# Graph network on one core: in the last layer one block of nodes passes from gathering to multiplication

## The chip, the cores and the metric

The kernel runs on one core of one Trainium2 chip. The metric is the device time of one execution in microseconds (us). The time before is 2127.4 us, the median of 3 runs (2123.55 to 2129.25).

## The reference

6250 nodes with 256 features (C) each, 100,000 edges from `src` to `dst`, random and sorted by `dst`. In short:

```python
h = relu(layernorm(x))                       # N = 6250, C = 256
y = h
for l in range(3):                           # three layers
    a = y + segment_sum(y[src], dst, N)      # each node adds up its neighbours
    a = relu(a @ W1s[l] + b1s[l])
    a = relu(a @ W2s[l] + b2s[l])
    y = a @ W3s[l] + b3s[l]
a = y + segment_sum(y[src], dst, N)          # the head, the last layer
a = relu(a @ cW1 + cb1)
a = relu(a @ cW2 + cb2)                      # cW2 is 256 x 64
return x + a @ cW3 + cb3                     # cW3 is 64 x 256
```

Everything is float32.

## The kernel before

**Blocks and layers.** The nodes are cut into 49 blocks of 128 (the last one holds 106). After a preparation (sorting the edges' indices, layernorm, a first split of the features) there are four layers, the head being the last. In each, every destination block needs the sum over its neighbours, its aggregate, which is made in one of two ways.

**Gathered blocks.** The edges of a block lie in 17 index columns of 128. For each column POOL issues one indirect DMA (`rows<-table,idx`, L1407) that fetches 128 rows of the layer's features from a table in memory. When all 17 are there a *visit* follows: 23 TensorE matmuls (46 records in the trace, since float32 is done in two passes) `sums<-rows,hot`, L1446, which add the rows up by destination with the help of one-hot matrices (`hot`, L1430, from DVE). DVE adds the sums to the node's own features (`u<-u,sums`, L1475), TensorE turns the result (L1506), and ACT adds the first bias and applies the relu. (The first weight of each layer is already in the features that are summed, since a sum and a matmul commute: the third weight of a layer has been multiplied with the first of the next.)

**Multiplied blocks.** For other blocks the kernel holds a count matrix, 6250 sources by 128 destinations, in uint8. It is cast to fp32r in strips (`a<-at`, by ACT and DVE in turn) and multiplied with the features, which lie in the tile `XY` for all 49 source blocks, split into a high and a low half. Four blocks together make a panel (L1700: 196 matmuls of 512 columns); a single block is multiplied "by node" (L1622: 49 matmuls, the strip being the stationary operand). Which block goes which way is told by `panels`, by `gone` (blocks that can be gathered) and by `solos`, the single blocks that a later layer multiplies. The first layer gathers 23 blocks and multiplies 26 by node; the second and third multiply seven panels and block 19 and gather 20 blocks; the last multiplies seven panels and blocks 18 and 19 and gathers 19.

**Building the matrices.** The 30 count matrices (blocks 18 to 47) are built once, during the first layer, in the order `made`. Each takes 16 *build steps* (GSUB): two matmuls `bp<-hi,lo` (L1094) of one-hot tiles that DVE makes (`lo` and `hi`, both L1053; one pair serves two steps, each has two buffers) and one copy of the counts into the uint8 tile `at`, by ACT (L1102) and DVE (L1104) in turn. A finished matrix is stored to memory (`mats`) for the later layers. There are three `at` tiles; a matrix is begun only when the casts of the one three places before it are written.

**Turns.** Products are written in turns, one strip of the matrix each: 13 a block by node, 49 a panel. Before a turn's matmuls stands whatever is due: a visit, a piece of a small network, and in the first layer up to three build steps, as far as an evenly rising list of goals asks and the buffers allow (`product_by_node`):

```python
goal = min(goals[at - PRE], built[0] + 3)
while built[0] < goal and free_of(built[0] // GSUB - 3):
    next(beside); built[0] += 1
```

**The plan of the gathers.** The order is fixed when the program is written. A planned clock adds up what TensorE is to do (`clock`, with prices for columns, visits and build steps). For each layer `work_of` estimates the work; the plan ends `TAIL[l]` planned us before that work does, and the gathers are spread evenly up to there (`pace`). Each gather waits on POOL for a matmul of its planned moment. A visit stands where the clock reaches its time, or, at the latest, `LATE[l]` turns past the layer's last turn (negative: before it):

```python
self.end = begun[self.l] + work_of(self.l) - TAIL[self.l]
self.pace = (self.end - clock[0] - MARGIN) / self.upto[-1]
...
return now[0] >= ends[self.l] + LATE[self.l] or clock[0] >= self.first + (
    self.upto[self.done + 1] - self.upto[1]) * self.pace
```

**The small networks.** For four blocks at a time (block 48 alone) there are two more matmuls, the *seconds* and the *thirds*. Before the head these are L1256 and L1313; in the head the seconds are `ps<-h,w`, L1248 for four blocks and L1256 for one, the thirds `ps<-clT,h`, L1268 for four and L1310 for one. In the head the input x is added: it is loaded into `xt` (L521, the load issued by SP; L1284 zeroes the tile first where block 48 does not fill it), DVE adds the bias to it (L1287) and the product (`zz`, L1297), and SP stores `zz`. For the last panel, blocks 44 to 47, the inputs are fetched ahead into `rows` tiles and L1280 adds the bias. The tile `clT` served the builds and is used again later as space (`spare`): for single blocks' aggregates and for the bias row, so that L1268, L1287 and L1310 name it as an operand.

**The queues.** Each engine takes its instructions in program order. Loads of matrices, of x and all stores are issued on SP's queue, gathers on POOL's.

Of the kernel before, what the change touches and what calls it, by code (L numbers as in the profile page):

```python
# [10 lines left out]
U8 = mybir.dt.uint8  # L11
# [6 lines left out]
P = 128  # L18
# [378 lines left out]
def sorted_edges(  # L397
# [39 lines left out]
    N, C = x.shape  # L437
    (E,) = src.shape
    NLAYER = W1s.shape[0]
# [27 lines left out]

    gone = [(0, 4), (4, 4), (8, 4), (12, 4), (16, 4), (44, 4), (48, 1)]
    panels = [(20, 4), (24, 4), (28, 4), (32, 4), (36, 4), (40, 4), (44, 4)]
    solos = [[], [19], [19], [18, 19]]  # L470
    stock = panels + [(b, 1) for b in max(solos, key=len)]
    place_of = {b + i: (p, i) for p, (b, n) in enumerate(stock) for i in range(n)}
    S0 = 2 * min(place_of)
# [3 lines left out]
    made = [b + i for b, n in teams for i in range(n)]  # L477
    for i in range(panels[-1][1]):
        made.insert(6 * i + 5, panels[-1][0] + i)
    assert sorted(made) == sorted(place_of) and sum(gone[-3]) == panels[0][0] and gone[-2] == panels[-1] and all(n == gone[0][1] for _, n in gone[:-1]) and sorted(  # L480
        b + i for b, n in gone[:-2] + gone[-1:] + panels for i in range(n)) == list(range(NT))
    NQ = len(gone)
# [498 lines left out]
    with tc.manual_schedule():  # L981
        with tc.tile_pool(name="prep", bufs=2) as prep, tc.tile_pool(
            name="ps_t", bufs=2, space=PSUM
# [374 lines left out]
        class Gathered:  # L1358
# [23 lines left out]
            def meets(self):  # L1382

                if self.first is None or self.done == self.n or now[0] < self.rest:
                    return False
                return now[0] >= ends[self.l] + LATE[self.l] or clock[0] >= self.first + (
                    self.upto[self.done + 1] - self.upto[1]) * self.pace

            def begin(self):
                self.one_hots(0)  # L1390
                self.end = begun[self.l] + work_of(self.l) - TAIL[self.l]
                self.pace = (self.end - clock[0] - MARGIN) / self.upto[-1]
# [121 lines left out]
        EARLY = 8  # L1514
        PRE = (GSUB + EARLY) // 2
        tails = [7] + [panels[-1][1] + gone[-1][1]] * (NLAYER - 1) + [panels[-1][1]]
        order = [[]] + [[0, 1, 2, 19, 3, 4, 5, 6]] * 2 + [[0, 1, 18, 2, 3, 19, 4, 5, 6]]
        order = [[p if p < len(panels) else place_of[p][0] for p in o] for o in order]
        nodes = [b + i for b, n in teams for i in range(n)]
        parts = [(j, 1) for j in range(NT)]  # L1520
# [11 lines left out]
        spare = clT.rearrange("p a q s -> p (a q s)").bitcast(F32)  # L1532
        sums = ps_g.tile([P, W], F32, name="sums")
        MARGIN = 6.0
        TAIL = [10.0] + [-5.0] * (NLAYER - 1) + [10.0]
        LATE = [-8] + [10] * (NLAYER - 1) + [-8]
        COLS, FULL32, TURN, VISIT, BUILD, BURST = 0.457e-3, 1.68e-3, 0.4, 3.0, 0.2, 0.3
        clock = [0.0]
        FAR, SPAN = 7, 6
# [9 lines left out]
        def work_of(l):  # L1549

            t = (len(nodes) if l == 0 else sum(stock[p][1] for p in order[l])) * NT * W * COLS
            t += len(layers[l].blocks) * (len(ROUNDS) * VISIT + TURN)
            for k, n in ((l, NT - tails[l]), (l - 1, tails[l - 1])):
                mid = NOUT if k == NLAYER else C
                t += (k >= 0) * n * (P * KC + C) * FULL32 * (2 if mid == C else 0.5)
            t += 2 * (len(gone) + (len(teams) if l == 0 else len(panels)) - 1) * BURST
            if l == 0:
                t += BUILD * GSUB * len(made) + TURN * len(nodes)
            return t
# [44 lines left out]
        def product_by_node(l, bs, ps_a, us, beside):  # L1604
            begun.setdefault(l, clock[0])
            aggs = [ps_a.tile([P, W], F32, name="agg") for _ in bs]
            for j0, m in solo_parts if l else node_parts[pieces.index(bs)]:
                at = now[0]
                tick(open_one(l))
                open_one(l).advance()  # L1610
                if beside is not None:
                    goal = min(goals[at - PRE], built[0] + 3)
                    while built[0] < goal and free_of(built[0] // GSUB - 3):
                        next(beside)
                        built[0] += 1
                prepare(at + 1 + (AHEAD if l == 0 else AHEAD + 2))
                a = ring.pop(at)
                for j in range(j0, j0 + m):
                    assert l == 0 or (l, j) in fresh
                    for i, agg in enumerate(aggs):  # L1620
                        d = (i * m + j - j0) * P
                        mm = nc.tensor.matmul(agg, a[:, d:d + P], XY[:, j, :], start=(j == 0),  # L1622
                                              stop=(j == NT - 1))
                        passed(W * COLS, mm)
                    if l == 0 and bs == pieces[-1]:
                        seen(l, j)

            def halves():
                for u, agg in zip(us, aggs):
                    nc.scalar.copy(u, agg[:, :C])  # L1630

            def whole():
                for u, agg in zip(us, aggs):
                    nc.vector.tensor_tensor(u, u, agg[:, C:], OP.add)  # L1634

            later(1, halves)
            later(2, whole)
# [39 lines left out]
        def product(l, p, ps_a):  # L1677
            b0, n = stock[p]
            if n == 1:
                k = solos[l][::-1].index(b0)  # L1680
                u = alone[l, b0] = late.tile([P, C], F32, name="us", bufs=1) if (
                    k == 1) else spare[:, k // 2 * C:(k // 2 + 1) * C]
                return product_by_node(l, (b0,), ps_a, [u], None)
            last = len(panels) - 1
            w = n * P
            begun.setdefault(l, clock[0])
            agg = [ps_a.tile([P, W], F32, name="agg") for _ in range(KC)]
            for at, j in enumerate(c * CH + i for c in CHUNKS for i in range(CH)):
                u = now[0]
                tick(open_one(l))  # L1690
                open_one(l).advance()
                if l == NLAYER and p == last and at == NT - 3:
                    bring_inputs(b0, n)
                prepare(u + 1 + AHEAD + 2)
                a = ring.pop(u)
                assert (l, j) in fresh, (l, j, now[0], ends[l - 1], [k for k in range(NT) if (l, k) not in fresh], len(queue), layers[l - 1].done)
                for c in range(KC):
                    for half in range(2):
                        o = half * C + c * P
                        mm = nc.tensor.matmul(agg[c][:, :w], XY[:, j, o:o + P], a[:, :w],  # L1700
                                              start=(at == 0 and half == 0),
                                              stop=(at == NT - 1 and half == 1))
                    passed(2 * w * COLS, mm)
                if p == last:
                    seen(l, j)
            h1 = work.tile([P, KC, W], F32, name="h1", bufs=2)
            hurry = p == last
            for c in range(KC):
                if hurry and c:
                    nc.vector.tensor_scalar(h1[:, c, :w], agg[c][:, :w], b1[l][:, c:c + 1], 0.0,  # L1710
                                            op0=OP.add, op1=OP.max)
                else:
                    nc.scalar.activation(h1[:, c, :w], agg[c][:, :w], AF.Relu,  # L1713
                                         bias=b1[l][:, c:c + 1])
            mlp(l, b0, n, h1, hurry, FAR)
# [12 lines left out]
        with tc.tile_pool(name="hots", bufs=1) as hots, tc.tile_pool(  # L1728
            name="ats", bufs=1
        ) as ats, tc.tile_pool(name="rings", bufs=AHEAD + 2) as rings, tc.tile_pool(  # L1730
            name="gath", bufs=24
        ) as gath, tc.tile_pool(
            name="ps_a", bufs=2, space=PSUM
        ) as ps_a, tc.tile_pool(name="ps_b", bufs=3, space=PSUM) as ps_b:
            begun = {0: clock[0]}
            rings.tile([P, 64], U8, name="align", bufs=1)
            layers[0].begin()
            layers[0].send(8)
            beside = build(hots, ats, ps_b)
            while now[0] < PRE:  # L1740
                for _ in range(2):
                    next(beside)
                    built[0] += 1
                tick(layers[0])
                layers[0].advance()
            later(1, lambda: later(2, lambda bad=verdict(): judge(bad)))
            for team in teams:
                product_of_team(*team, ps_a, beside, team == teams[-1])
            assert next(beside, None) is None and built[0] == total
        chunks = ctx.enter_context(tc.tile_pool(name="chunks", bufs=1))  # L1750
        late = ctx.enter_context(tc.tile_pool(name="late", bufs=1))
        rings = ctx.enter_context(tc.tile_pool(name="rings2", bufs=AHEAD + 5))
        rings.tile([P, 128], U8, name="align", bufs=1)
        gath = ctx.enter_context(tc.tile_pool(name="gath2", bufs=27))
        ps_a = ctx.enter_context(tc.tile_pool(name="ps_a2", bufs=4, space=PSUM))
        for l in range(1, NLAYER + 1):
# [67 lines left out]
```

## Time and profile before

| | |
|---|---|
| median of 3 runs | 2127.4 us |
| the profiled execution's own time | 2128.1 us |
| its span | 2126.3 us |
| PE (TensorE matmul) busy | 2034.3 us, 96% |
| PEld (weight load) busy | 1495.9 us, 70% |
| DVE busy | 925.0 us, 44% |
| ACT busy | 872.8 us, 41% |
| POOL busy | 1445.9 us, 68% |
| gathers (L1407) | 1394, 996 ns each on POOL |
| products: panels (L1700), by node (L1622) | 978.6 us, 405.4 us of PE |
| visits (L1446) | 248.3 us of PE, 33.5 us idle before them |
| build matmuls (L1094) | 128.3 us of PE, 14.9 us idle before them |

A view of a stretch gives window, length, and then the busy time of PE, PEld, DVE, ACT and POOL (with the number of instructions), the mean granted TensorE clock, the DMA engines' busy share and GB/s. A view of waits gives, for a group, its idle time in us, how many waits, and the longest. A timeline row gives start, duration, engine, line, operation, tiles (out<-in), number of instructions, and in brackets the idle time before it and what ended it. The first layer's products by node run from 150 to 689 us; the second layer's gathers begin at 714 us, the third's at 1195, the last's at 1668; the last product ends at 2116. What stands ahead of 150 us is the preparation.

### The profile page before, as it was taken

The page shows a single profiled execution, that of the slowest core. Times are in us where ns is not written, and L with a number is a line of the kernel's source. Part 1 is how long each engine was busy: PE and PEld are TensorE (multiplying, and loading weights), DVE is VectorE, ACT ScalarE, POOL GpSimd, SP SyncE. Part 2 cuts the span into 40 slices and gives each one's busy share as a digit, 9 for nine tenths or more (in the row PEclk, how much of TensorE's full clock was granted, in tenths as well). Part 3 has the DMA queues.
Part 4 walks back from the last instruction along what each step waited for, and adds up shares of the span by engine and source line. Part 5 has one row for each costly group of instructions (what it writes and reads, how often), then busy time and mean ns, then how long its engine had stood idle before and what let it go on. Part 6 is the DMA issues. An engine that isn't in the chain of part 4 may idle for free.

```text
span 2126.3 us, 33236 instructions
## 1 busy us (share of the span) xinstructions
PE 2034.3 (96%) x12076; PEld 1495.9 (70%) x12076; DVE 925.0 (44%) x2103; ACT 872.8 (41%) x1793; POOL 1445.9 (68%) x1467
## 2 busy tenths in 40 slices
PE   6889999999999999999999999999999999989998
PEld 4657676667676777777777777777776767766665
DVE  6987767677662422232234322322233323223333
ACT  5766656456555433323233423232233322222222
POOL 3747777677774477777777477777776477777772
PEclk9989999999999999999999999999999999999999
DMA  5534455545455654555566554555555555555563
GB/s 174 159 117 148 145 156 150 157 139 162 140 161 168 205 163 145 160 177 161 154 184 202 171 165 149 176 166 158 169 171 176 173 170 185 161 184 185 154 189 109
DMA packets 184900, 347.54 MB, mean 163 GB/s; under 512 B 32446, under 2 KB 118496, under 8 KB 184726
## 3 DMA queue, kind: packets, MB, share of 16 engines
q0 software_dynamic: 68960, 185.36, 29.9%
q1 hardware_dynamic: 113838, 158.12, 22.8%
q8 instruction: 96, 1.57, 0.3%
q10 hardware_dynamic: 1928, 1.85, 0.3%
q14 instruction: 78, 0.64, 0.1%
HBM read 287.93 MB, written 57.26 MB: 162 GB/s over the span
## 4 chain that ended last, share of the span: by engine, by line
PE 86%; DMA 4%; DVE 3%; issue 1%; ACT 1%; POOL 1%; DVEq 0%; SPq 0%; POOLq 0%; ACTq 0%
PE agg L1700 43%; PE agg L1622 15%; PE sums L1446 11%; PE ps L1256 6%; PE ps L1313 6%; PE bp L1094 4%; DMA rows<-table,idx 4%; PE ps L1506 1%; DVE hi L1053 1%; POOL rows L1407 1%; DVE at L1104 1%; PE ps L1268 1%; PE ps L1248 0%; DVE lo L1053 0%; ACT at L1102 0%
## 5 line engine op out<-in xcount | busy, mean ns | idle before, releaser
L1407 POOL DMA_INDIRECT rows<-table,idx x1394 | 1388.8, 996 | 595.7 <-issue 225.7
L1700 PE MATMUL agg<-a,XY 128*128 128x512 f32 x4116 | 978.6, 395 | 1.9 <-DVE clT L1634 1.9
L1700 PEld LDWEIGHTS agg<-a,XY 128*128 128x128 f32 x4116 | 764.9, 188 | 192.7 <-issue 35.0
L1598 ACT CAST a<-at 128x512 fp32r<-128x512 uint8 (+1 forms) x542 | 328.7, 617 | 653.7 <-PE agg L1700 613.1
L1598 DVE CAST a<-at 128x512 fp32r<-128x512 uint8 x543 | 246.8, 456 | 515.7 <-PE agg L1700 479.1
L1622 PE MATMUL agg<-XY,a 128*128 128x512 f32 x1470 | 405.4, 410 | 1.7 <-ACT a L1582 1.0
L1622 PEld LDWEIGHTS agg<-XY,a 128*128 128x128 f32 x1470 | 260.0, 190 | 51.4 <-issue 6.6
L1446 PE MATMUL sums<-rows,hot 128*32 128x256 f32 x3772 | 248.3, 391 | 33.5 <-DMA rows<-table,idx 33.3
L1446 PEld LDWEIGHTS sums<-rows,hot 128*32 128x32 f32 x3772 | 124.0, 111 | 151.0 <-DMA rows<-table,idx 46.1
L1582 ACT CAST a<-at 128x512 fp32r<-128x512 uint8 (+2 forms) x362 | 197.2, 576 | 6.6 <-PE agg L1622 6.6
L1102 ACT CAST at<-bp 128x392 uint8<-128x392 f32 x252 | 121.5, 490 | 186.9 <-PE bp L1094 181.3
L1104 DVE CAST at<-bp 128x392 uint8<-128x392 f32 x228 | 128.6, 564 | 137.4 <-PE bp L1094 135.0
L1475 DVE TENSOR_TENSOR u<-u,sums 128x256 f32<-128x256 f32 x82 | 34.4, 419 | 301.3 <-PE agg L1700 273.6
L1094 PE MATMUL bp<-hi,lo 128*128 128x196 bf16 x960 | 128.3, 256 | 14.9 <-DVE hi L1053 13.3
L1313 PE MATMUL ps<-w,h 128*128 128x256 f32 x588 | 133.8, 379 | 1.4 <-ACT h L1259 0.9
L1053 DVE TENSOR_TENSOR hi<-cols,pairs 128x784 bf16<-128x784 bf16 x240 | 134.9, 562 | 0.0
L1256 PE MATMUL ps<-h,w 128*128 128x512 f32 (+3 forms) x332 | 133.8, 545 | 0.3 <-ACT h L1713 0.3
L1094 PEld LDWEIGHTS <-lo 128*128 128x128 bf16 x960 | 72.3, 100 | 83.5 <-DVE hi L1053 34.9
L1313 PEld LDWEIGHTS ps<-w,h 128*128 128x128 f32 x588 | 111.3, 190 | 18.5 <-ACT h L1259 1.4
L1321 DVE TENSOR_TENSOR zz<-ps,w 128x512 f32<-128x512 f32 (+1 forms) x75 | 50.2, 679 | 116.5 <-PE ps L1313 116.5
L1053 DVE TENSOR_TENSOR lo<-lanes,pairs 128x512 bf16<-128x512 bf16 x240 | 100.6, 419 | 0.7 <-issue 0.3
L1510 ACT ACTIVATE h<-ps,bias 128x256 f32<-128x256 f32 (+1 forms) x116 | 47.6, 464 | 128.5 <-PE ps L1506 128.5
(170 smaller groups left out, 962.6 us busy)
## 6 DMA issues: line engine op xcount, KB each, us to landing
at<-mat SPq DMA_DIRECT2D x151, 448.0 KB
mat<-at SPq DMA_DIRECT2D x30, 784.0 KB
rows<-table,idx POOLq DMA_INDIRECT x1394
table<-zz SPq DMA_DIRECT2D x72, 256.0 KB
back<-table SPq DMA_DIRECT2D x99, 128.0 KB
xs<-in_x_dram SPq DMA_DIRECT2D x8, 768.0 KB
table<-zs SPq DMA_DIRECT2D x24, 256.0 KB
out_dram<-zz SPq DMA_DIRECT2D x24, 256.0 KB
```

The lines of the kernel that those rows point to most:

```text
L1053: nc.vector.tensor_tensor(o.rearrange("p q (n t) -> p q n t", t=2), values.rearrange("p (n t) -> p n t", t=2)[:, None, :, :].to_broadcast( ...
L1094: mm = nc.tensor.matmul(bp[:, m * HW:(m + 1) * HW], lo[:, q + m, :], hi[:, q + m, :], start=True, stop=True)
L1102: nc.scalar.copy(o, v)
L1104: nc.vector.tensor_copy(o, v)
L1256: mm = nc.tensor.matmul(ps[:mp, :w], weights[l][0][:, c, i * P:i * P + mp], h1[:, c, :w], start=(c == 0), stop=(c == KC - 1))
L1313: mm = nc.tensor.matmul(o, h2[0][:, c, nodes], w3[:, c, :], start=(c == 0), stop=(c == KC - 1))
L1407: got = nc.gpsimd.indirect_dma_start(out=t, out_offset=None, in_=tables[self.l][:, :], in_offset=bass.IndirectOffsetOnAxis(ap=idx[:, o:o + ...
L1446: nc.tensor.matmul(self.sums[m * Q:(m + 1) * Q, :C], self.hot[:, c - min(rounds), m, :], self.rows[g, c + 4 * m], start=(c == ROUNDS[0][0] ...
L1582: nc.scalar.copy(a[:, i * m * P:(i + 1) * m * P].rearrange("p (j d) -> p j d", j=m), counts[b][:, j:j + m, :])
L1598: cast(o, at[:, :, d:d + m * P])
L1622: mm = nc.tensor.matmul(agg, a[:, d:d + P], XY[:, j, :], start=(j == 0), stop=(j == NT - 1))
L1700: mm = nc.tensor.matmul(agg[c][:, :w], XY[:, j, o:o + P], a[:, :w], start=(at == 0 and half == 0), stop=(at == NT - 1 and half == 1))
```

## The change

In the last layer block 17 is no longer gathered but multiplied by itself, as blocks 18 and 19 already are: 18 blocks are gathered and three multiplied singly. Its count matrix is built in the first layer, as the 27th of now 31 (`made.insert(26, 17)`). In the last layer's order its product stands after the first panel and block 18's after the second. `work_of` counts the added product, the visit that goes and the added build steps of itself. Four numbers of the plan change: the first layer's plan ends 16 planned us before its work (10 before), the last layer's 3 us after it (10 before it), and the last layer's last visit is forced 5 turns ahead of the products' end instead of 8. The aggregate of the third single block takes another slot of `spare`. `clT` grows by 128 bytes a partition for the two half blocks of 17, and the alignment tiles are changed to suit.

```diff
     panels = [(20, 4), (24, 4), (28, 4), (32, 4), (36, 4), (40, 4), (44, 4)]
-    solos = [[], [19], [19], [18, 19]]
+    solos = [[], [19], [19], [17, 18, 19]]
...
         made.insert(6 * i + 5, panels[-1][0] + i)
+    made.insert(26, 17)
...
-        order = [[]] + [[0, 1, 2, 19, 3, 4, 5, 6]] * 2 + [[0, 1, 18, 2, 3, 19, 4, 5, 6]]
+        order = [[]] + [[0, 1, 2, 19, 3, 4, 5, 6]] * 2 + [[0, 17, 1, 18, 2, 3, 19, 4, 5, 6]]
...
-        TAIL = [10.0] + [-5.0] * (NLAYER - 1) + [10.0]
-        LATE = [-8] + [10] * (NLAYER - 1) + [-8]
+        TAIL = [16.0] + [-5.0] * (NLAYER - 1) + [-3.0]
+        LATE = [-8] + [10] * (NLAYER - 1) + [-5]
...
                 u = alone[l, b0] = late.tile([P, C], F32, name="us", bufs=1) if (
-                    k == 1) else spare[:, k // 2 * C:(k // 2 + 1) * C]
+                    k == 1) else spare[:, 3 * (k // 2) * C:(3 * (k // 2) + 1) * C]
...
-            rings.tile([P, 64], U8, name="align", bufs=1)
+            rings.tile([P, 192], U8, name="align", bufs=1)
...
-        rings.tile([P, 128], U8, name="align", bufs=1)
```

How the builds stand in the first layer is seen on ACT, around the last strip of the fourteenth block's product. `a<-at` 128x512 is one turn's cast, `at<-bp` is ACT's half of the evictions, so one for every two build steps, `pairs` begins half a matrix, and `un` takes up a finished product. (Lines of the changed kernel count one more here.) Before:

```order
L1582 COPY a<-at 128x128
L1048 COPY pairs<-clT 128x64
L1102 COPY at<-bp 128x49x8
L1582 COPY a<-at 128x512 x2
L1102 COPY at<-bp 128x49x8
L1582 COPY a<-at 128x512
L1630 COPY un<-agg 128x256
L1102 COPY at<-bp 128x49x8
L1582 COPY a<-at 128x512
L1102 COPY at<-bp 128x49x8
```

The same place of the changed kernel:

```order
L1583 COPY a<-at 128x512 x6
L1583 COPY a<-at 128x128
L1049 COPY pairs<-clT 128x64
L1103 COPY at<-bp 128x49x8 x2
L1583 COPY a<-at 128x512
L1103 COPY at<-bp 128x49x8
L1583 COPY a<-at 128x512
L1103 COPY at<-bp 128x49x8
L1049 COPY pairs<-clT 128x64
L1103 COPY at<-bp 128x49x8
```

Before, evictions and casts alternate nearly one to one; now seven casts stand without an eviction, and then five evictions follow with two casts among them.

The end of the last layer on PE: `agg<-a,XY` are the last panel's products, `sums<-rows,hot` the last visit, `ps` the small networks, `h_...` their operands (a number is only the tile's own). Before:

```order
L1248 MATMUL ps<-h_20413,w_16837 64x256 x4
L1700 MATMUL agg<-a,XY 128x512 x12
L1268 MATMUL ps<-clT,h_20534 128x256 x4
L1700 MATMUL agg<-a,XY 128x512 x12
L1256 MATMUL ps<-h_20522,w_16837 64x128 x2
L1700 MATMUL agg<-a,XY 128x512 x8
L1310 MATMUL ps<-clT,h_20595 128x256
L1700 MATMUL agg<-a,XY 128x512 x20
L1248 MATMUL ps<-h_20651,w_16837 64x256 x4
L1268 MATMUL ps<-clT,h_20654 128x256 x4
```

And now, from the last visit on:

```order
L1447 MATMUL sums<-rows,hot 32x256 x23
L1701 MATMUL agg<-a,XY 128x512 x8
L1507 MATMUL ps<-ident,u 128x128 x2
L1701 MATMUL agg<-a,XY 128x512 x4
L1249 MATMUL ps<-h_20600,w_16940 64x256 x4
L1701 MATMUL agg<-a,XY 128x512 x12
L1269 MATMUL ps<-clT,h_20715 128x256 x4
L1257 MATMUL ps<-h_20705,w_16940 64x128 x2
L1311 MATMUL ps<-clT,h_20763 128x256
L1249 MATMUL ps<-h_20742,w_16940 64x256 x4
L1269 MATMUL ps<-clT,h_20779 128x256 x4
```

From the last visit on 24 product matmuls remain where 64 did, and the thirds of blocks 16 to 19, the seconds and thirds of block 48 now stand behind the last product.

On DVE, at the same place, before:

```order
L1287 TENSOR_TENSOR xt<-xt,clT 128x512 x2
L1598 COPY a<-at 128x512
L1297 TENSOR_TENSOR zz<-ps,xt 128x512 x2
L1598 COPY a<-at 128x512 x2
L1284 MEMSET xt 128x256
L1287 TENSOR_TENSOR xt<-xt,clT 128x256
L1297 TENSOR_TENSOR zz<-ps,xt 128x256
L1710 TENSOR_SCALAR h_20651<-agg,bias 128x512
L1280 TENSOR_TENSOR rows<-rows,clT 128x256 x4
L1297 TENSOR_TENSOR zz<-ps,rows 128x256 x4
```

And now:

```order
L1711 TENSOR_SCALAR h_20742<-agg,bias 128x512
L1288 TENSOR_TENSOR xt<-xt,clT 128x512 x2
L1298 TENSOR_TENSOR zz<-ps,xt 128x512 x2
L1285 MEMSET xt 128x256
L1288 TENSOR_TENSOR xt<-xt,clT 128x256
L1298 TENSOR_TENSOR zz<-ps,xt 128x256
L1281 TENSOR_TENSOR rows<-rows,clT 128x256 x4
L1298 TENSOR_TENSOR zz<-ps,rows 128x256 x4
```

The relu of the last product (`h<-agg,bias`) now stands ahead of the adds of blocks 16 to 19 and of block 48, and all of these follow the last product.

## Prediction

> **What bounds the kernel now.** I read the page, then busy time by stage, the visits (the 46 "sums" records of one gathered block), PE's waits, POOL's gathers and the timeline of the first layer.
>
> ```profile
> 163.00:640.00 477.00, 468.53 (x3208) 330.39 (x3208) 337.10 (x763) 281.61 (x636) 349.04 (x349) 1.00 0.50 150
> 1690.00:2098.00 408.00, 381.66 (x2323) 279.24 (x2322) 124.02 (x253) 113.59 (x202) 303.41 (x306) 0.98 0.56 173
> ```
> Columns: window, length, busy PE, PEld, DVE, ACT, POOL, granted clock, DMA share, GB/s. In the first layer (upper row) PE is busy 98% and DVE 71%. In the last layer PE loses 26 us, and its clock is under 1.00.
>
> ```profile
> 730.00:1174.00 444.00, 56.56 (x920) 28.98 (x920) 1.00 0.56 170
> 1210.00:1642.00 432.00, 58.57 (x920) 29.66 (x920) 1.00 0.55 168
> 1690.00:2098.00 408.00, 66.57 (x874) 31.42 (x874) 0.98 0.56 173
> ...
> PE sums L1446 <- DMA rows<-table,idx: 26.0, 11, 6.2
> ...
> PE sums L1446 <- DMA rows<-table,idx: 4.9, 3, 1.7
> ...
> 1865.17 0.63 PE L1446 MATMUL sums<-rows,hot 128*32 128x256 f32 x6
> 1871.99 5.16 PE L1446 MATMUL sums<-rows,hot 128*32 128x256 f32 x40 [6.19 <-DMA rows<-table,idx]
> ...
> 1872.00:1877.00 5.00, 5.00 (x40) 2.12 (x40) 0.00 (x0) 0.00 (x0) 2.40 (x3) 0.51 0.67 231
> ```
> The first three rows are PE's time in visits (second, third, last layer). The second layer's 20 cost 56.56/20 = 2.83 us each. The last layer's 19 should take 53.8; they took 66.57 and waited 26.0 besides, so 38.8 us are lost to late rows. A third of that is no idle time: after a wait of 6.19 the other 40 matmuls took 5.16 us, at a granted clock of 0.51. The third layer lost 58.57 - 56.6 + 4.9 = 6.9.
>
> [...]
>
> Why rows are late:
>
> ```profile
> 714.25 4.41 POOL L1407 DMA_INDIRECT rows<-table,idx  x1 [43.75 <-ACT XY L1185]
> ...
> 1170.56 2.80 PE L1446 MATMUL sums<-rows,hot 128*32 128x256 f32 x46
> ...
> 1194.88 1.28 POOL L1407 DMA_INDIRECT rows<-table,idx  x1 [26.13 <-PE agg L1700]
> ...
> 1636.37 0.63 PE L1446 MATMUL sums<-rows,hot 128*32 128x256 f32 x6
> ...
> 1668.41 0.95 POOL L1407 DMA_INDIRECT rows<-table,idx  x1 [31.85 <-PE agg L1700]
> 1669.66 0.95 POOL L1407 DMA_INDIRECT rows<-table,idx  x1 [0.30 <-issue]
> ...
> 2091.71 0.97 POOL L1407 DMA_INDIRECT rows<-table,idx  x1 [0.31 <-issue]
> ...
> 2094.35 2.80 PE L1446 MATMUL sums<-rows,hot 128*32 128x256 f32 x46
> ```
> A gather costs POOL 0.95 + 0.30 = 1.25 us at best. From the last layer's first gather to its last visit PE has 2094.35 - 1668.41 - 38.8 = 387 us of work for 323 gathers: 1.20 each, which POOL cannot follow. The same for the layers of 20 visits and 340 gathers: (1636.37 - 1194.88 - 6.9)/340 = 1.28 in the third (loss 6.9), (1170.56 - 714.25)/340 = 1.34 in the second (none).
>
> **Last layer.** The product of block 17 is added: 49 matmuls, as this one of block 18.
>
> ```profile
> 1762.61 8.12 PE L1622 MATMUL agg<-XY,a 128*128 128x512 f32 x35
> ...
> 1772.11 3.49 PE L1622 MATMUL agg<-XY,a 128*128 128x512 f32 x14
> ```
> That is +11.4 us after overlap at the ends. A visit goes, -2.8, with its 17 gathers. Casts and `mat` loads of the new product lie beside PE: DVE and ACT are busy 124 and 114 of 408 us there. PE's work up to the last visit becomes 405 us, since the visit now stands 24 product matmuls ahead of the end where 64 stood: 405/306 = 1.32 a gather, against POOL's 1.25. Between the third layer's loss and the second's none, nearer the latter, I keep 2 us (ends 0 and 8). So the stall gives -36.8.
>
> **The end.** Three pieces of MLP that stood among the last panel's products now follow them: thirds of blocks 16 to 19 (1.13), seconds and thirds of block 48 (0.65, 0.70). The products end 2.5 us earlier for it. What follows them gets longer:
>
> ```profile
> 2107.86 0.27 DVE L1284 MEMSET xt<- 128x256 f32 x1
> 2108.16 0.76 SPq L521 DMA_DIRECT2D xt<-in_x_dram  x2
> ...
> 2110.41 0.43 DVE L1287 TENSOR_TENSOR xt<-xt,clT 128x256 f32<-128x256 f32 x1 [2.27 <-DMA xt<-in_x_dram]
> ...
> 2111.51 4.85 PE L1700 MATMUL agg<-a,XY 128*128 128x512 f32 x20
> 2111.61 0.42 DVE L1297 TENSOR_TENSOR zz<-ps,xt 128x256 f32<-128x256 f32 x1 [0.78 <-PE ps L1310]
> ...
> 2116.47 0.75 DVE L1710 TENSOR_SCALAR h<-agg,bias 128x512 f32<-128x512 f32 x1 [4.43 <-PE agg L1700]
> 2117.13 1.42 DVE L1280 TENSOR_TENSOR rows<-rows,clT 128x256 f32<-128x256 f32 x4
> 2119.72 1.42 DVE L1297 TENSOR_TENSOR zz<-ps,rows 128x256 f32<-128x256 f32 x4 [1.17 <-PE ps L1268]
> ```
> Before, DVE's last add ends at 2121.14, 4.8 us after the products (2116.36), and the kernel 5.2 later. Now, in DVE's order, there stand behind the products: 0.75 (h), two pairs of adds of blocks 16 to 19 (2 x 1.29), MEMSET 0.27, the wait for block 48's x (2.28 from the MEMSET's end), 0.43, 0.42, and the two groups of four (2 x 1.42): 9.7 us with the first 0.1, +4.9. The load of x is issued only after that MEMSET and, on SP, behind two stores of blocks 16 to 19, so about 1 more (an estimate; ends 0 and 3): +5.9.
>
> **First layer.** The 31st matrix is 16 build steps more (two bp matmuls, half of DVE's `lo` and `hi`, one eviction). In 13 turns a block, PE and DVE look like this:
>
> ```profile
> 327.49 3.01 PE L1622 MATMUL agg<-XY,a 128*128 128x512 f32 x12
> ...
> 330.34 0.69 PE L1094 MATMUL bp<-hi,lo 128*128 128x196 bf16 x6
> ...
> 331.71 0.95 DVE L1430 TENSOR_TENSOR hot<-colf,rel 128x768 f32<-128x768 f32 x1
> 331.82 0.34 PE L1094 MATMUL bp<-hi,lo 128*128 128x196 bf16 x2
> 333.06 0.56 DVE L1104 CAST at<-bp 128x392 uint8<-128x392 f32 x1
> 333.19 0.51 PE L1094 MATMUL bp<-hi,lo 128*128 128x196 bf16 x4 [1.03 <-DVE hi L1053]
> ...
> 334.34 0.56 DVE L1104 CAST at<-bp 128x392 uint8<-128x392 f32 x1
> 334.50 0.51 PE L1094 MATMUL bp<-hi,lo 128*128 128x196 bf16 x4
> ...
> 335.62 0.56 DVE L1104 CAST at<-bp 128x392 uint8<-128x392 f32 x1
> ...
> PE bp L1094 <- DVE hi L1053: 7.2, 12, 1.4
> ```
> Three turns without a step take PE 330.34 - 327.49 = 2.85, 0.95 each; one with two steps 1.31 (333.19 to 334.50). A step is thus 0.18 of PE, and the matrix 16 x 0.18 = +2.9. DVE needs 1.28 for two steps (one eviction to the next, back to back), 0.64 a step. A turn of two steps fits (1.28 in 1.31); one of three asks 1.92 of DVE against 0.95 + 3 x 0.18 = 1.49 of PE. The two turns of three that begin at 330.34 end at 334.50: 4.16 instead of 2.98, 0.59 lost a turn.
>
> Before, 8 of the layer's turns have three steps; counted over the whole order, now 69 have, in runs of up to 10, behind runs without any. The goal rises faster, the builder stops at its third buffer and then catches up three steps a turn. It is no more DVE work than 12 us, but it is bunched: in the empty turns DVE cannot work ahead, as `lo` and `hi` have two buffers. So 61 more such turns cost between 0.43 (DVE's bare rate) and 0.59 (measured, with a `hot` in between) each, 26 to 36 us; where a visit or MLP lies in the run PE waits less, which stretches the lower end to 15. I take 0.57, 35 us: in long runs DVE has its other work to do too.
>
> The layer's last visit was forced two planned microseconds after its last gather:
>
> ```profile
> 668.05 0.63 PE L1446 MATMUL sums<-rows,hot 128*32 128x256 f32 x6
> 671.07 4.46 PE L1446 MATMUL sums<-rows,hot 128*32 128x256 f32 x40 [2.38 <-DMA rows<-table,idx]
> ```
> It lasts 668.05 to 675.53, 7.5 instead of 2.8. With the plan ending sooner 8 lie between: -4.6. The second and third layers keep their order: 0. The 128 bytes by which tiles move: 0, as nothing in the trace depends on them.
>
> **Sum.** 2.9 + 35 - 4.6 - 36.8 + 11.4 - 2.8 - 2.5 + 5.9 = +8.5. The profiled execution took 2128.1 (span 2126.3), 0.7 over the median of the runs, 2127.4; from the median: 2136.
>
> **Rivals.**
> Bunching costs less: the runs of three fall beside visits and MLPs, whose 2.8 to 3.5 us of PE let DVE catch up. At 15 to 26 us the kernel takes 2116 to 2127. For it: 30% of PE's time in that layer is no product. Against: the runs stand in turns with products alone at least as often.
>
> Faster, because DVE has room: at 71% busy and 12 us more it stays under 74%, so the steps are absorbed wherever they stand. With the bursts at 5 or less, 2136 - 30 = 2106. It decides below 20 us of new waits for `hi`. [...] Against it stands DVE back to back for the 1.28 us above, with PE waiting for it in a layer whose mean is 71%.
>
> Gathers stay late: bulk loads share the DMA engines, and a row asked for in a full stretch lands late although POOL has time. In the visit at 1865.17 PE waited beyond 1871 for gathers sent before it. At the third layer's 6.9 or a little more, and a tail 3 us longer, 2143 to 2149.
>
> **Chances.** Forecast (2130 to 2142) 0.52; less bunching 0.23; room on DVE 0.10; late gathers as well 0.15. The measurement tells no change within 0.3%, 6.4 us: 2121.0 to 2133.8. Slower is late gathers and most of the forecast, 0.61; faster is the DVE rival and the low part of less bunching, 0.12; same the rest, 0.27. The range 2120 to 2148 leaves out the DVE rival and the ends of its neighbours.
>
> **What would show it.** Right: PE's wait for DVE `hi` in the first layer rises from 7.2 us to over 35, and that layer (last visit at 668 now) gets 30 to 38 longer; visits of the last layer take near 2.83 with waits under 8; the last add ends some 10 us after the last product. Wrong: waits for `hi` under 20 (then faster), waits for rows over 15 in the last layer (then slower still), or second and third layers that change by more than 2 us.

## The result and the profile after

The changed kernel takes 2139.6 us (median; 2138.6 to 2141.0) against 2125.5 of the kernel before: 1.0062 of it, 95% interval 1.0046 to 1.0077, so 10 to 16 us slower. The forecast was 2136 with a range of 2120 to 2148, and slower. The profiled execution's span went from 2126.3 to 2137.7, by 11.4; the table splits this by marks that both traces have (the first layer's products begin at 150 us in both).

| stretch | before | after | change | forecast |
|---|---|---|---|---|
| 150 us to the beginning of the first layer's last visit | 518.05 | 557.88 | +39.8 | +37.9 |
| that visit | 7.48 | 2.80 | -4.7 | -4.6 |
| to the end of the third layer's last visit | 965.98 | 967.46 | +1.5 | 0 |
| to the end of the kernel | 484.8 | 459.6 | -25.2 | -24.8 |

Busy time by stretch in the first layer (window, length, then busy PE, PEld, DVE, ACT, POOL, granted clock, DMA share, GB/s), before:

```profile
150.00:668.05 518.05, 508.89 (x3438) 360.93 (x3437) 355.39 (x804) 310.56 (x715) 378.05 (x377) 1.00 0.51 153
```

After, with PE's waits in the same stretch:

```profile
150.00:707.88 557.88, 521.81 (x3469) 367.53 (x3469) 365.45 (x828) 316.90 (x724) 382.85 (x379) 0.99 0.48 144
```

```profile
PE bp L1095 <- DVE hi L1054: 33.9, 52, 2.0
```

PE was idle for 9.2 us of that stretch and is now for 36.1; 26.7 of the 26.9 more is the wait for DVE's `hi` (7.2 before). DVE's busy share has fallen over the same stretch, from 355.4/518.1 = 69% to 365.5/557.9 = 66%, while PE waits for DVE nearly five times as long. The other 12.9 of the 39.8 us PE was busier (521.81 against 508.89); the half clock shown below is some 5 of them. The timeline of one such place, PE and then DVE:

```profile
588.45 1.17 PE L1623 MATMUL agg<-XY,a 128*128 128x512 f32 x4
589.47 0.34 PE L1095 MATMUL bp<-hi,lo 128*128 128x196 bf16 x2
589.97 0.51 PE L1095 MATMUL bp<-hi,lo 128*128 128x196 bf16 x4 [0.16 <-DVE hi L1054]
590.26 1.17 PE L1623 MATMUL agg<-XY,a 128*128 128x512 f32 x4
591.68 0.52 PE L1095 MATMUL bp<-hi,lo 128*128 128x196 bf16 x4 [0.25 <-DVE hi L1054]
594.16 0.34 PE L1095 MATMUL bp<-hi,lo 128*128 128x196 bf16 x2 [1.97 <-DVE hi L1054]
```

```profile
588.54 0.57 DVE L1105 CAST at<-bp 128x392 uint8<-128x392 f32 x1 [4.95 <-PE bp L1095]
...
591.54 0.56 DVE L1105 CAST at<-bp 128x392 uint8<-128x392 f32 x1
592.02 1.28 DVE L1322 TENSOR_TENSOR zz<-ps,w 128x512 f32<-128x512 f32 x2
593.21 0.42 DVE L1054 TENSOR_TENSOR lo<-lanes,pairs 128x512 bf16<-128x512 bf16 x1
593.54 0.56 DVE L1054 TENSOR_TENSOR hi<-cols,pairs 128x784 bf16<-128x784 bf16 x1
```

DVE stood idle for 4.95 us ahead of 588.54, with nothing to build; from there on it works back to back and PE waits: 0.16, 0.25, and 1.97 when a small network's adds (`zz`, 1.28) stand ahead of the next one-hots.

The clock is 0.99 over the stretch because it was halved three times, behind waits of 1.69, 1.64 and 1.97. Around the first:

```profile
322.00:323.00 1.00, 0.50 (x5) 0.93 0.85 298
323.00:326.00 3.00, 3.00 (x11) 0.50 0.64 189
326.00:327.00 1.00, 1.00 (x5) 0.86 0.00 0
```

(Window, length, PE's busy time, granted clock.) Some 1.7 us of full speed are lost each time (0.07 + 1.5 + 0.14), about 5 of the layer's 39.8. PE was not idle throughout ahead of the first stretch: the wait was 1.69, and PE worked for 1.16 of the 3.41 us before it (its row stands in the last section).

In the last layer the visits hardly wait any more. PE's time in them, and its waits there, after:

```profile
1690.00:2120.00 430.00, 52.62 (x828) 26.48 (x828) 1.00 0.57 178
```

```profile
PE sums L1447 <- DMA rows<-table,idx: 1.5, 3, 0.8
```

18 visits at 2.83 would take 50.9; with 1.7 more and 1.5 of waits the loss is 3.2, where 38.8 were lost (forecast 2). The end, on PE and then on DVE:

```profile
2118.29 3.01 PE L1701 MATMUL agg<-a,XY 128*128 128x512 f32 x12
2121.24 1.13 PE L1269 MATMUL ps<-clT,h 64*128 64x256 f32 x8
2124.02 0.65 PE L1257 MATMUL ps<-h,w 128*64 128x128 f32 x4 [1.65 <-DVE zz L1298]
...
2126.33 1.97 PE L1249 MATMUL ps<-h,w 128*64 128x256 f32 x8
2128.94 2.08 PE L1269 MATMUL ps<-clT,h 64*128 64x256 f32 x8 [0.63 <-ACT h L1253]
```

```profile
2121.42 0.75 DVE L1711 TENSOR_SCALAR h<-agg,bias 128x512 f32<-128x512 f32 x1 [5.67 <-PE agg L1701]
2122.08 1.28 DVE L1288 TENSOR_TENSOR xt<-xt,clT 128x512 f32<-128x512 f32 x2
2123.28 1.28 DVE L1298 TENSOR_TENSOR zz<-ps,xt 128x512 f32<-128x512 f32 x2
2124.57 0.27 DVE L1285 MEMSET xt<- 128x256 f32 x1
2127.52 0.42 DVE L1288 TENSOR_TENSOR xt<-xt,clT 128x256 f32<-128x256 f32 x1 [2.68 <-DMA xt<-in_x_dram]
...
2131.05 1.42 DVE L1298 TENSOR_TENSOR zz<-ps,rows 128x256 f32<-128x256 f32 x4 [1.18 <-PE ps L1269]
```

From the last product (2121.30) to the last add (2132.47) are 11.2 us, 4.8 before: +6.4 where +5.9 was forecast. Two steps were not foreseen. Block 48's seconds (L1257) wait 1.65 for a PSUM buffer that the `zz` of blocks 16 to 19 must first read. And from about 2125 the clock is halved (window, length, PE's busy time, clock):

```profile
2125.00:2131.00 6.00, 5.18 (x18) 0.51 0.39 124
```

So the last seconds (L1249) take 1.97 us instead of the 1.08 of the eight L1249 ahead of them, and DVE's last add waits 1.18 us for the thirds behind them.

### The profile page after: what moved, and what is told of

It is laid out like the page before. It is cut to its first block, busy times and chain, and to the rows that moved or that the text cites. A ratio compares the mean times of both kernels' runs of the same rounds, so it can differ in the third digit from the quotient of the medians.

```text
span 2137.7 us, 33382 instructions
## 1 busy us (share of the span) xinstructions
PE 2045.0 (96%) x12111; PEld 1509.4 (71%) x12111; DVE 938.6 (44%) x2133; ACT 884.6 (41%) x1811; POOL 1435.5 (67%) x1450
## 5 line engine op out<-in xcount | busy, mean ns | idle before, releaser
L1599 ACT CAST a<-at 128x512 fp32r<-128x512 uint8 (+1 forms) x549 | 333.0, 617 | 630.9 <-PE agg L1701 588.6
L1599 DVE CAST a<-at 128x512 fp32r<-128x512 uint8 (+1 forms) x550 | 251.1, 458 | 522.2 <-PE agg L1701 475.8
L1623 PE MATMUL agg<-XY,a 128*128 128x512 f32 x1519 | 414.7, 410 | 1.7 <-ACT a L1583 1.0
L1623 PEld LDWEIGHTS agg<-XY,a 128*128 128x128 f32 x1519 | 272.5, 191 | 56.1 <-issue 8.3
L1447 PE MATMUL sums<-rows,hot 128*32 128x256 f32 x3726 | 232.4, 381 | 7.1 <-DMA rows<-table,idx 7.1
L1105 DVE CAST at<-bp 128x392 uint8<-128x392 f32 x236 | 133.1, 564 | 154.6 <-PE bp L1095 126.1
L1447 PEld LDWEIGHTS sums<-rows,hot 128*32 128x32 f32 x3726 | 119.0, 109 | 114.5 <-issue 28.4
L1095 PE MATMUL bp<-hi,lo 128*128 128x196 bf16 x992 | 135.4, 257 | 42.3 <-DVE hi L1054 39.8
L1054 DVE TENSOR_TENSOR hi<-cols,pairs 128x784 bf16<-128x784 bf16 x248 | 139.7, 563 | 0.0
L1257 PE MATMUL ps<-h,w 128*128 128x512 f32 (+3 forms) x332 | 134.3, 547 | 2.0 <-DVE zz L1298 1.7
```

Source lines behind the costliest of these rows:

```text
L1054: nc.vector.tensor_tensor(o.rearrange("p q (n t) -> p q n t", t=2), values.rearrange("p (n t) -> p n t", t=2)[:, None, :, :].to_broadcast( ...
L1095: mm = nc.tensor.matmul(bp[:, m * HW:(m + 1) * HW], lo[:, q + m, :], hi[:, q + m, :], start=True, stop=True)
L1105: nc.vector.tensor_copy(o, v)
L1257: mm = nc.tensor.matmul(ps[:mp, :w], weights[l][0][:, c, i * P:i * P + mp], h1[:, c, :w], start=(c == 0), stop=(c == KC - 1))
L1447: nc.tensor.matmul(self.sums[m * Q:(m + 1) * Q, :C], self.hot[:, c - min(rounds), m, :], self.rows[g, c + 4 * m], start=(c == ROUNDS[0][0] ...
L1599: cast(o, at[:, :, d:d + m * P])
```

## Experiments on the first layer

Three theories of the 39.8 us. *Bunching*: 61 more turns with three build steps, in which DVE can't keep up. *Load*: the 31st matrix is more work for DVE than it has room for, however it stands. *Gathers*: the first layer's plan ends sooner, and its denser gathers disturb it.

**e1: at most two steps a turn.** The changed kernel with

```diff
-                    goal = min(goals[at - PRE], built[0] + 3)
+                    goal = min(goals[at - PRE], built[0] + 2)
```

> The changed kernel with at most two build steps a turn instead of three: no turn has three (69 had), 236 have two (129 had), the number of steps is the same. Bunching theory: a turn of two asks 1.28 us of DVE in 1.31 of PE, so PE's wait for hi falls from 33.9 to 15 us or less, the first layer's last visit begins at 671 to 685 instead of 707.9, and the time is 2103 to 2117. Load theory (the 31st matrix's own work on DVE is the cost, however it stands): waits stay near 34, time within 5 of 2139.6. Gather theory (the first layer's tighter plan is the cost): the same, within 5 of 2139.6.

**e2: the 31st matrix built last.** The changed kernel with

```diff
-    made.insert(26, 17)
+    made.insert(30, 17)
...
-        goals = [min(g0 + (total - g0) * u // u1, total) for u in range(1, steps + 1)]
+        most = total - GSUB
+        goals = [min(g0 + (most - g0) * u // u1, most) + max(0, min(u - u1, GSUB)) for u in range(1, steps + 1)]
```

> The changed kernel with block 17's matrix as the 31st and last built, one step a turn in the last 25 turns, which have no build step otherwise; the goals of the first 30 matrices are those of before, and 8 turns have three steps, as before. Bunching theory: waits for hi 7 to 10 us, last visit of the first layer at 668 to 674, time 2101 to 2107. Load theory: 16 steps more are still there, waits above 25, time above 2130. Gather theory: the plan still ends sooner, time within 5 of 2139.6.

**e3: bunching alone, in the kernel before.** The goals reach their end eleven turns sooner (297; the expectation says ten and 298):

```diff
-        g0, u1 = GSUB + EARLY, steps - len(node_parts[-1]) - AHEAD - 1
+        g0, u1 = GSUB + EARLY, steps - len(node_parts[-1]) - AHEAD - 12
```

> The kernel before, with one thing changed: the goals of the builder reach their end 10 turns sooner (298 instead of 308). No matrix more, the last layer as before; 77 turns with three steps instead of 8. Bunching theory: 69 such turns at 0.60 us, +41, first layer's last visit near 709, waits for hi 35 to 42, time 2155 to 2172. Load theory: no work is added, time within 4 of before. Gather theory: the plan of the gathers is untouched, time within 4 of before.

**e4: the first layer's plan as it was.** The changed kernel with

```diff
-        TAIL = [16.0] + [-5.0] * (NLAYER - 1) + [-3.0]
+        TAIL = [10.0] + [-5.0] * (NLAYER - 1) + [-3.0]
```

> The changed kernel with the first layer's plan ending 10 planned us before its work again, not 16. Last send and last visit of that layer are then 1.3 planned us apart instead of 8. Bunching theory: waits for hi stay at 31 to 36; the last visit waits for rows again, +3 to +6, time 2142 to 2146. Gather theory: the first layer gets 25 to 40 us shorter, time 2100 to 2115. Load theory: as the bunching theory.

Measured, on one chip (the kernel before took 2128.6 there):

| | time, us | of before (95% interval) | turns with three | last visit begins | PE's wait for `hi` |
|---|---|---|---|---|---|
| before | 2128.6 | 1 | 8 | 668.05 | 7.2 |
| after (beside 2125.5 of the kernel before) | 2139.6 | 1.0062 (1.0046 to 1.0077) | 69 | 707.88 | 33.9 |
| e1 | 2114.4 | 0.9930 (0.9914 to 0.9947) | 0 | 681.78 | 15.0 |
| e2 | 2102.9 | 0.9882 (0.9866 to 0.9899) | 8 | 669.75 | 6.3 |
| e3 | 2164.5 | 1.0172 (1.0155 to 1.0188) | 77 | 703.27 | 37.0 |
| e4 | 2135.6 | 1.0032 (1.0017 to 1.0046) | 69 | 698.87 | 30.6 |

The row of waits in e1, e2 and e3 (each a view of its own):

```profile
PE bp L1095 <- DVE hi L1054: 15.0, 24, 1.5
```

```profile
PE bp L1095 <- DVE hi L1054: 6.3, 14, 1.1
```

```profile
PE bp L1094 <- DVE hi L1053: 37.0, 52, 2.0
```

Load falls: e2 has all the 31 matrices and waits no more than the kernel before; its last visit begins 1.7 us later, which is all that the matrix costs (2.9 forecast). Gathers falls with it: e2 keeps the sooner plan of the first layer, and its time is 2102.9. e3 has no matrix more, and its layer is 35 us longer. Bunching holds in both directions: 69 more turns of three cost 35.2 in e3, 0.51 each. In the changed kernel 61 cost 39.8 - 1.7 = 38.1, or 33 without the three stretches of half clock, 0.54 each. Most of that price is the wait itself, 29.8/69 = 0.43 in e3 and 26.7/61 = 0.44 in the changed kernel; in the rest PE is busier. e3 waits as long, and its clock stays at 1.00 in this stretch.

e1 says that a turn of two does not quite fit either. Its builder still stops at the third buffer (runs of four or five turns without a step) and then makes two steps in every turn for a long stretch; the waits are 15.0 and the layer is 12 us longer than e2's. What matters is that steps stand evenly, not only how many a turn may hold.

e4 is a miss. The last visit waits 2.31 us for its rows again, as expected, yet the time did not rise by 3 to 6: by the ratios it fell by 0.003, some 6 us, with intervals that just touch. In the traces the layer's last visit begins 9.0 us earlier than after; of that 3.3 are shorter waits for `hi`, and 5 are the three stretches of half clock, which are not there (up to that visit the clock is 1.00 in e4 and 0.99 after; the mean clock of all executions says the same: 0.988 to 0.990 after, 0.991 to 0.992 in e4). The visits of e4 stand some planned us later than after's, and so lie elsewhere among the runs of three. Whether it is this alone is asked below (e11).

## Experiments on the last layer

The next four kernels ran on a chip on which the kernel before took 2369 us, with PE often held up by nothing that the profile shows (51.1 us ahead of the visits in e5); so they are compared there only with the kernel before, and three of them were run again. All but e8 and e12 start from e2, whose first layer is undisturbed.

**e5 and e10: the last layer's plan as it was.**

```diff
-        TAIL = [16.0] + [-5.0] * (NLAYER - 1) + [-3.0]
-        LATE = [-8] + [10] * (NLAYER - 1) + [-5]
+        TAIL = [16.0] + [-5.0] * (NLAYER - 1) + [10.0]
+        LATE = [-8] + [10] * (NLAYER - 1) + [-8]
```

> The kernel with the 31st matrix built last (e2), and the last layer's two plan numbers as they were: its plan ends 10 planned us before its work (3 after, in e2) and the last visit is forced 8 turns ahead of the end (5). The last visit then stands 60 or so product matmuls before the end, and block 48's seconds and thirds stand among the products again. Theory that the late plan's tail costs what it saves in stalls: the end after the last product falls from 16.4 to about 10 us, the gathers get 1.28 of PE's work each, as in the third layer, and the visits lose 6 to 9 us instead of 4: time within 4 of e2's. Rival (the late plan is what removes the stall): the loss comes back to 20 or more, time 12 or more over e2.

**e6: half way.** As e5, with 4.0 in place of 10.0.

> As e5, with the plan ending 4 planned us before the work (half way). Tail theory: loss in the visits 4 to 7, end as in e5 or up to 2 longer, time from 4 under e2 to 2 over. Rival: loss 10 or more, time 5 or more over e2.

**e7 and e11: the first layer's plan as it was**, 16.0 back to 10.0 as in e4, without the runs of three.

> e2 with the first layer's plan ending 10 planned us before its work, not 16: what e4 did to the changed kernel, here without the runs of three steps. If e4's gain of about 6 came from where its visits fell among the runs of three, it is gone here and the last visit's stall is back: +2 to +5 against e2, waits for hi unchanged at 6 to 8. If the tighter plan costs something by itself, -4 to -8 against e2.

**e8 and e12: the kernel before, one block's gathers left out.**

```diff
+                free = [g for g, (b, n, i, _) in enumerate(self.blocks) if l == NLAYER and b + i == 17]
-                self.order = [(g, k) for g, rounds in self.visits for k in self.tiles(rounds)]
+                self.order = [(g, k) for g, rounds in self.visits for k in self.tiles(rounds) if g not in free]
...
-                for _, rounds in self.visits:
-                    self.upto.append(self.upto[-1] + len(self.tiles(rounds)))
+                for g, rounds in self.visits:
+                    self.upto.append(self.upto[-1] + len(self.tiles(rounds)) * (g not in free))
...
-                                self.hot[:, c - min(rounds), m, :], self.rows[g, c + 4 * m],
+                                self.hot[:, c - min(rounds), m, :], self.rows.get((g, c + 4 * m), self.rows.get((g - 1, T - 1))),
```

> The kernel before, where the last layer's visit of block 17 asks for no rows of its own and uses an old tile in place of them (so block 17's sums are left out of the result). 306 gathers instead of 323, all matmuls as before; PE has 387/306 = 1.265 us of work a gather. Theory that POOL cannot follow at 1.20 (it needs 1.25): the loss of 38.8 falls to between 6 and 15, waits for rows to 5 to 10, time 24 to 33 under before. Rival (rows are late because they share the DMA engines with the bulk loads, whatever the count): the loss falls with the visits' number at most, by 2, time within 4 of before.

Against 2369 of the kernel before on that chip: e5 2350 (0.9924, 0.9896 to 0.9953), e6 2346 (0.9911, 0.9879 to 0.9942), e7 2348 (0.9907, 0.9875 to 0.9939), e8 2343 (0.9886, 0.9846 to 0.9926). They don't tell e5, e6 and e7 apart, and what the half-way plan of e6 is worth stays open. Run again:

> The kernel of e2 once more, as the yardstick of e10 to e12 on the same chip (e5 to e8 ran on a chip on which the kernel before took 2369 us, so that they can't be set against e2). Bunching theory: 0.988 of before, as e2; waits for hi 6 to 8 us.

> The kernel of e5: e9 with the last layer's two plan numbers of before. Tail theory (the late plan's longer end costs what it saves in stalls): the end after the last product 10 to 11 us instead of 16, the visits lose 6 to 9 us, time within 4 of e9. Rival (the late plan is what removes the stall): visits lose 20 or more, time 12 or more over e9.

> The kernel of e7: e9 with the first layer's plan ending 10 planned us before its work. In the changed kernel itself that gained 6 (e4), of which 5 were three stretches of half clock after waits for hi of 1.6 to 2.0 us, and 3 less waiting for hi, against a last visit that waits 2.3 again. If that gain hangs on the runs of three steps, here it is +2 to +5; if the tighter plan costs by itself, -4 to -8.

> The kernel of e8: before, with the last layer's visit of block 17 asking for no rows. Theory that POOL cannot follow at 1.20 us of PE a gather (now 1.265, it needs 1.25): the 38.8 us lost in the visits fall to between 6 and 15, time 24 to 33 under before. Rival (the rows are late for the DMA engines they share, whatever their number): time within 4 of before.

| | time, us | of before (95% interval) |
|---|---|---|
| before | 2128.8 | 1 |
| e9 (e2 again) | 2101.1 | 0.9879 (0.9862 to 0.9896) |
| e10, last layer's plan as it was | 2101.7 | 0.9870 (0.9855 to 0.9885) |
| e11, first layer's plan as it was | 2105.9 | 0.9891 (0.9875 to 0.9906) |
| e12, before without one block's gathers | 2105.1 | 0.9893 (0.9877 to 0.9909) |

**e12** speaks for POOL's rate. 17 gathers fewer out of 323, with every matmul in place, give 23.7 us. Its visits in the last layer (window, length, PE's time, PEld's) and PE's waits there:

```profile
1690.00:2098.00 408.00, 59.53 (x874) 28.97 (x874) 1.00 0.55 171
```

```profile
PE sums L1447 <- DMA rows<-table,idx: 9.2, 8, 3.9
```

19 visits should take 53.8: the loss is 5.7 + 9.2 = 14.9, against 38.8, at the upper end of the 6 to 15 that I expected. It is 23.9 less, which is the fall in time, 23.7, just short of the 24 to 33 expected. The rival that rows are late for the transfers beside them, whatever their number, had allowed 2.

That POOL was short of time is also seen on POOL itself, from the kernel before's first gather of the last layer to its last visit (count, busy time, mean ns, idle time):

```profile
L1407 POOL DMA_INDIRECT rows<-table,idx x323 | 319.9, 990 | 136.2 <-PE agg L1700 71.9 <-issue 50.9 <-DMA rows<-table,idx 5.8
```

Of the 136.2 us idle, 31.8 lie ahead of the first gather and 0.30 ahead of each other one, which leaves 7.8. A gather took POOL 0.99 + 0.30 = 1.29 us on average, not the 1.25 at best by which the prediction reckoned: 323 of them are 417 us, beside 387 us of PE's work. So 30 of the 38.8 us are POOL's bare rate.

**e10** shows that the last layer's two plan numbers are worth nothing that these runs can tell. Its visits and waits:

```profile
1660.00:2110.00 450.00, 54.31 (x828) 27.50 (x828) 0.99 0.55 172
```

```profile
PE sums L1447 <- DMA rows<-table,idx: 4.5, 2, 3.4
```

The loss is 54.31 - 50.9 + 4.5 = 7.9, e9's 6.0 (53.01 - 50.9 + 3.9); from the last product to the last add it takes 4.8 us, as before the change, and e9 10.0. The late plan bought a smaller stall with a longer end, and the times are equal. So the whole gain of the last layer comes from the block that is multiplied.

Put in a row, the layers give loss against PE's work a gather: 38.8 us at 1.20, 14.9 at 1.26 (e12: from 1669.58 to 2069.32, for 306), 6.9 at 1.28, 7.9 at 1.29 (e10: from its first gather at 1668.35 to its last visit at 2071.34, without the loss, for 306), 3.2 at 1.31 (after; the same plan in e9 lost 6.0), none at 1.34. It grows as PE's work falls below POOL's mean of 1.29: the shortfall times the number of gathers gives 30 of the 38.8 and 10 of the 14.9. What lies beside that, 9 us of the 38.8 and 3 to 8 us near 1.29, is not explained further.

**e11** is the plan's number in a quiet first layer. Its last visit, and e9's:

```profile
670.01 0.63 PE L1447 MATMUL sums<-rows,hot 128*32 128x256 f32 x6
672.46 2.78 PE L1447 MATMUL sums<-rows,hot 128*32 128x256 f32 x40 [1.82 <-DMA rows<-table,idx]
```

```profile
671.10 2.80 PE L1447 MATMUL sums<-rows,hot 128*32 128x256 f32 x46
```

The visit waits again and lasts 5.23 instead of 2.80, but it begins sooner: the end of the visit is 1.3 us later. The medians differ by 4.8 and the ratios by 0.0012 (2.6 us), with intervals that overlap. The sooner plan is worth at most 5 us here, which is not clear of the noise; in the changed kernel, among the runs of three, it was worth nothing or less (e4). That e4's gain hangs on these runs fits both, but no run moved the visits alone, so it stays argued.

**A version that beats both** is e2 (e9): 2101 to 2103 us, 0.988 of the kernel before and, by the two ratios, 0.982 of the changed one, 38 us. It is the same change with block 17's matrix, which the first layer doesn't need, built in eight of the last 25 turns, which had no steps (two steps in every second turn, where the expectation says one a turn). With the last layer's plan as it was (e10) it is as fast.

## Why the prediction was right

- **Late rows in the last layer, -36.8**: held. The loss went from 38.8 to 3.2 (2 assumed). e12 and POOL's row show the cause; the rate to be met is POOL's mean, 1.29, not 1.25. The time to the end of the kernel from the third layer's last visit changed by -25.2, the terms for it sum to -24.8.
- **Product 17, +11.4, the visit, -2.8, and the end, -2.5 + 5.9**: from the third layer's last visit to the last product, PE's work by node grew from 23.5 to 35.4 us (+11.9), the visits with their waits fell from 92.6 to 54.1 (-38.5 for -39.6), and the pieces that moved behind the products took 2.7 out; 1.7 less in the panels' products was not forecast. The end's longer part measured +6.4, near the forecast in part by luck: without the half clock, in e9 (its last L1249 took 1.08 us, not 1.97), it is 10.0 - 4.8 = +5.2. That the late plan's end cancels what it saves was not seen: the prediction priced the two in different terms and took both as given.
- **The matrix, +2.9, and bunched builds, +35**: together 37.9 for 39.8. The cause is shown by e2 and e3. The size was right for a mixed reason: 0.57 a turn was taken. 0.51 to 0.54 was measured, of which 0.43 to 0.44 is the wait, DVE's bare rate as the prediction had it, and three stretches of half clock, about 5 us, make up the rest. The prediction had these stretches only in the visits, so that the sum came out this near is in part luck. Two of its signs were narrowly missed: the waits for `hi` are 33.9 where over 35 was forecast, and the stretch is 39.8 longer where it was 30 to 38.
- **The statement that a turn of two steps fits** (1.28 of DVE in 1.31 of PE): too simple. It holds for single turns; in long runs DVE's other work stands between, and e1 still waited 15.0.
- **The first layer's last visit, -4.6**: -4.7 in the trace, but as a price for the plan's number it failed. Of the 4.7, 2.4 were the wait, and the visit's slow matmuls (40 in 4.46 us, in e11 in 2.78) most of the rest; to undo it cost at most 5 us in a quiet layer (e11) and gained some 6 in the changed kernel (e4). What moving 23 visits does elsewhere in the layer was left out.
- **Second and third layers, 0**: +1.5, of which 0.7 are waits for rows (5.6 against 4.9).
- **The rivals**: less bunching fell, by 38.1 us where it had 15 to 26. Room on DVE fell, by 26.7 us of new waits for `hi` where it needed under 20. Late gathers fell, by 1.5 us of waits for rows in the last layer. DVE's busy share, by which the second argued, went down while the waits rose.

## What to carry to other kernels

A producer with few buffers, like DVE with two of `hi` here, has no use for its idle time (4.95 us ahead of 588.54, then PE waited 0.16, 0.25 and 1.97): what counts is the work that a consumer asks for in one turn against what the producer makes in that turn, and a busy share averaged over the stage (66%, with 33.9 us of waits) did not show it here. When one more unit is added to such a pipeline, look at where the pacing now meets the buffer limit, and put units that nobody waits for where the producer is idle. A stream of small transfers is a rate to be met: a gather took POOL 1.29 us on average, nothing was lost at 1.34 us of PE's work a gather and 38.8 us at 1.20, and the shortfall of each one, summed, gives 30 of these. To take away one transfer in nineteen was worth 23.7 us here, and to move two numbers of their plan was worth nothing that shows.

## What the runs showed of the hardware

After PE waits of 1.64 to 1.97 us the granted clock was 0.50 for one stretch of 3.41 us in the changed kernel's first layer, three times. The stretches begin at 322.87, 473.05 and 595.93 us, 44 and 36 times 3.413 us apart. In the kernel before, stretches of half clock begin at 671.96, 1736.92, 1870.04 and 1982.68, 312, 39 and 33 times 3.413 us apart. So in each of the two traces they lie on one grid of 3.413 us. With the changed kernel's first layer cut into windows of that grid (window, length, PE's busy time, clock), the three windows in which PE worked least are the three ahead of these stretches. The next, with 1.82 us of work, is followed by full speed:

```profile
319.45:322.87 3.42, 1.16 (x10) 1.00 0.49 152
469.64:473.05 3.41, 1.49 (x10) 1.00 0.87 274
592.52:595.93 3.41, 1.63 (x10) 1.00 0.96 285
438.92:442.33 3.41, 1.82 (x12) 1.00 0.26 77
```

In e3 a wait of 1.97, from 594.75 to 596.72, was followed by full speed. With windows that meet at 595.86, in the middle of the wait, PE worked for 2.16 us in one and for 2.42 in the other:

```profile
592.45:595.86 3.41, 2.16 (x15) 1.00 0.34 91
595.86:599.27 3.41, 2.42 (x15) 1.00 0.81 256
```

So a wait of 1.97 us cost 2 us in e3 and, with the half clock behind it, 3.7 in the changed kernel, where 1.64 of it (592.52 to 594.16) lay in one window of the grid. That the lie of a wait on the grid decides it is an argument; no run moved a wait alone. Nor do the windows divide by PE's work alone: in the changed kernel one with 1.63 us of work was followed by a clock of 0.50, and in the kernel before one with 1.57 (at 1822.25) by 1.00.
